# Attention and quantised FFN on one core: K's and Q's products ahead of the scores in the first five units, 27 turns of the identity instead of 30

## The chip, the core and the metric

The kernel runs on one core of one Trainium2 chip. The metric is the device time of one execution in microseconds (us). The core has five engines that run side by side, each taking its own instructions strictly in the order in which they stand: PE (TensorE, matmuls, with PEld for its weight loads), DVE (VectorE), ACT (ScalarE), POOL (GpSimd) and SP, which here issues all DMA transfers. Engines wait for each other through semaphores.

## The reference

The input x has 16 sequences of 256 tokens with 256 channels. One attention layer and one feed-forward layer follow, each with a layer norm before and after it and a residual. Cut to what matters here:

```python
x = x + layernorm(attn(layernorm(x)))     # 16 heads of 128, causal
    q = einsum('bpd,hde->bphe', x, W_Q) + b_Q      # the same for k, v
    scores = einsum('bqhe,bkhe->bhqk', q, k) / sqrt(128), masked above the diagonal
    z = einsum('bkhe,bhqk->bqhe', v, softmax(scores))
    out = einsum('bqhe,hed->bqd', z, W_O) + b_O
x = x + layernorm(ffn(layernorm(x)))      # gate, up, down, weights in 4-bit codes with scales
```

The results are wanted in float32 accuracy. The kernel gets it from TensorE's faster float32r format by splitting each operand into a high part and a low part (high = value rounded to float32r, low = value minus high) and adding three products: high x high, high x low, low x high.

## The kernel before, in words

**Tiles.** The 4096 tokens are worked in 8 blocks of 512 (two sequences each). Per block there are 8 pairs of heads, so 16 heads; one head in one block is a *unit*, and there are 128 units. After all units come the groups of the feed-forward layer. This case plays in the first units.

**What a unit u does**, stage by stage (the functions stand below):
- `st_qk` (L370): K's product `pk` (six matmuls of 128x512) and Q's product `pq` (six more). ACT copies from them `kh`, `kr`, `qh`, `qr` (with bias), DVE makes the low parts `kl`, `ql`. `pk` and `pq` have one PSUM buffer each: the next unit's `pk` waits until this unit's `kl` has read the old one, the next `pq` until `ql` has.
- `st_s` (L421): the scores, ten matmuls into two buffers `sc` (one for each sequence); DVE adds the mask and takes the row minimum `mn` (four instructions, with an accumulator read after each); then come the low parts of V that are waiting in the list `after` (L442); ACT takes four exponentials `pr` with their sums, DVE reciprocals `rc`, POOL scales `pr`. The next unit's scores need the two `sc` buffers, which the exponentials read last.
- `st_t` (L460): DVE's transpose `tr` within 32x32 squares, which waits for POOL's scaled `pr`; `st_w` and `st_b` (L471, L475) send it to DRAM (`hop`) and fetch it back (`pt`), which completes the transpose.
- `st_v` (L402): V's product `pv` for four heads at once; units 0 to 3 of each half block make the four parts. For the first two, ACT copies `vh` and the subtraction that gives `vl` is put into the list `after`, that is, it is issued on DVE by the *next* unit's `st_s`, behind its mask instructions. For the other two ACT copies `vr`. `pv` has one PSUM buffer.
- `st_p`, `st_z`, `st_o`: the splits `ph` and `pl` of `pt`, the product with V (`pz`), and the product with W_O (`po`).

**Weights.** Raw weights of a pair (`raw`, six buffers) are split once, in block 0, by `w_split` (L297): ACT writes the high part, DVE (for `wk`, `wq`) or POOL (for `wv`, `wo`) the low part; the splits are stored to DRAM and fetched back in later blocks. `w_split` also asks for the next pair's raw weights. `w_get` (L331) puts a split into the list `splits`; `slot` (L133) takes one job from such a list at fixed points of the loop, only a job of the kinds that it is asked for, and only the first of the list.

**Order.** `run` (L95) issues every compute instruction behind all earlier ones, so the order in which the Python code calls is the order on each engine; `dma` (L86) does the same for SP. At most eight transfers are under way, since each reuses the semaphore of the eighth before it.

**The start.** PE first turns the identity 30 times into an unused buffer (`keep_warm(30)`, L992), then transposes block 0's normalised tokens (`tpx`, with 3 and 6 more turns), and the loop of L1006 begins at i = -5. In step i the loop works on unit i+4's scores, unit i+5's K and Q, unit i's `pz`, and so on. Before step -5 the splits of pair 2 of V and pair 1 of K and Q are in the list (L998). Thus the order on PE in the first units is: pk0 pq0, sc0, pk1 pq1, pv0, sc1, pk2 pq2, pv1, sc2, ... (the number is the unit).

Of the kernel before, what the change touches and what calls it, by code (L numbers as in the profile page):

```python
# [28 lines left out]
def kernel(  # L29
# [30 lines left out]
    def f(ap):  # L60
        return ap.bitcast(F32)
# [43 lines left out]
    V_, G_, A_, N_ = "vgan"  # L105
    urgent, behind, splits, idle, made, spare = (deque() for _ in range(6))
# [18 lines left out]
    def add(jobs, job, kind):  # L125
        jobs.append([job, 0, kind])

    def overdue(time):
        while late and late[0][0] <= time:
            _, do, args = late.popleft()  # L130
            do(*args)

    def slot(kinds, *lanes):  # L133

        now[0] += 1
        overdue(now[0])
        for jobs in lanes or (splits, urgent, behind, made, spare, idle):
            if step(jobs, kinds):
                return
# [149 lines left out]
    def w_tile(n):  # L289
        return wp.tile([P, 2, 1024 if n == "v" else 512], F32R, tag=f"w{n}", name=f"w{n}", bufs=2)  # L290
# [36 lines left out]
    def split(p, n):  # L327
        w_split(p, n)
        yield from ()

    def w_get(p, n):  # L331

        if p < NG:
            add(splits, split(p, n), A_ if n in "vo" else V_)
        elif p < len(pairs):
            overdue(now[0] + 4)
            if n == "v":
                key, part = p // 2, p % 2
                w = HALF.pop(key) if part else w_tile(n)
                HALF[key] = w  # L340
                dma(f(w[:, part]), WD[key % (NG // 2), n][:, part])
                if part:
                    W[key, n] = w_view(HALF.pop(key))
            else:
                w = w_tile(n)
                dma(f(w), WD[p % NG, n])
                W[p, n] = w_view(w)
# [16 lines left out]
    N = len(units)  # L364
# [5 lines left out]
    def st_qk(i):  # L370
        b, g, j = units[i]
        h = 2 * g + j
        await_(ready, (1, b), urgent)
        await_(W, (i // 2, "k"), splits)
        await_(W, (i // 2, "q"), splits)
        xt = XT[1, b]
        wk_, wq_ = W[i // 2, "k"], W[i // 2, "q"]
        cols = slice(j * E, (j + 1) * E)
        pk = ps.tile([P, TB], F32, tag="pk", name="pk")
        mm3(pk, [(lambda a, kt=kt: wk_[:, a, kt, cols], lambda c, kt=kt: xt[:, c, kt, :]) for kt in range(2)], MOVING_LAST, lows_last=True)  # L380
        kh = work.tile([P, TB], F32R, tag="kh", name="kh")
        kl = work.tile([P, TB], F32R, tag="kl", name="kl")
        kr = work.tile([P, 2, P], F32, tag="kr", name="kr")
        bias = bqk[:, 1, h : h + 1]
        run(nc.scalar.activation, kh, pk, AF.Identity, bias=bias)
        run(nc.scalar.activation, kr, pk.rearrange("p (a c) -> p a c", a=2)[:, :, 0:P], AF.Identity, bias=bias)
        run(nc.vector.scalar_tensor_tensor, kl, pk, bias, f(kh), ALU.add, ALU.subtract)
        K[i] = (kh, kl, kr)

        pq = ps.tile([P, TB], F32, tag="pq", name="pq")  # L390
        mm3(pq, [(lambda a, kt=kt: wq_[:, a, kt, cols], lambda c, kt=kt: xt[:, c, kt, :]) for kt in range(2)], MOVING_LAST, lows_last=True)
        qh = work.tile([P, 2, P], F32R, tag="qh", name="qh")
        ql = work.tile([P, 2, P], F32R, tag="ql", name="ql")
        qr = work.tile([P, 2, P], F32, tag="qr", name="qr")
        bias = bqs[:, h : h + 1]
        pq2 = pq.rearrange("p (a c) -> p a c", a=2)
        run(nc.scalar.activation, qh, pq2[:, :, P:], AF.Identity, bias=bias)
        run(nc.scalar.activation, qr, pq2[:, :, 0:P], AF.Identity, bias=bias)
        run(nc.vector.scalar_tensor_tensor, ql, pq2[:, :, P:], bias, f(qh), ALU.add, ALU.subtract)
        Q[i] = (qh, ql, qr)  # L400
# [70 lines left out]
    def st_w(u):  # L471
        HOP[u] = dram.tile([P, 4, 6 * 32], F32, tag="hop", name="hop", bufs=4)
        spread(HOP[u], TR.pop(u).rearrange("p k m i -> p k (m i)"))
# [218 lines left out]
    def x_ops(sb):  # L692

        xr = []
        for b in (2 * sb, 2 * sb + 1):
            xr.append(wide("xr"))
            dma(xr[-1], HOP2[b])
        yield A_, 8

        def block(kt, bb):  # L700
            return xr[bb].rearrange("p a (m i) -> p m a i", m=8)[:, 4 * kt : 4 * kt + 4]

        def four(ap):
            return ap.rearrange("p (t a i) -> p t a i", t=4, a=4)

        ops = X[sb] = {}

        def put(name, hi, lo, src):
            run(nc.scalar.copy, four(hi), src)
            run(nc.gpsimd.tensor_tensor, four(lo), src, f(four(hi)), ALU.subtract)  # L710
            ops[name] = hi, lo

        def pair():
            t = work.tile([P, 2, 2, TB], F32R, tag="xT", name="xT", bufs=4)
            return [(t[:, 0, k], t[:, 1, k]) for k in range(2)]

        def less(o, a, b):
            run(nc.gpsimd.tensor_tensor, o, a, b, ALU.subtract)

        x11, x12, x21, x22 = block(0, 0), block(0, 1), block(1, 0), block(1, 1)  # L720
        p1, p2 = pair()
        put("11", *p1, x11)
        yield A_
        put("21", *p2, x21)
        yield G_
        t1, t3, t4 = x11, x12, x21
        less(t1, x12, x11)
        yield G_
        less(t3, x22, x12)
        yield G_  # L730
        t2 = four(sb_tile("raw", "xsum", 6))
        less(t2, x22, t1)
        yield A_
        p1, p2 = pair()
        put("t2", *p1, t2)
        yield G_
        less(t4, t2, x21)
        yield A_
        put("t1", *p2, t1)
        yield A_  # L740
        w = w_tile("k")
        put("t3", w[:, 0], w[:, 1], t3)
        yield A_
        w = w_tile("q")
        put("22", w[:, 0], w[:, 1], x22)

        def last_one():
            hi = work.tile([P, TB], F32R, tag="ph", name="xh")
            lo = work.tile([P, TB], F32R, tag="pl", name="xl")
            put("t4", hi, lo, t4)  # L750

        if sb == 0:

            ops["last"] = last_one
        else:
            yield A_
            last_one()
# [230 lines left out]
    def keep_warm(count):  # L988
        for n in range(count):
            run(nc.tensor.transpose, warm[:, n % 4, :], ident, ident)  # L990

    keep_warm(30)  # L992
    add(urgent, first, V_)
    finish(urgent)
    run(nc.gpsimd.tensor_scalar, bqs, bqk[:, 0, :], qscale, 1.0, ALU.mult, ALU.mult)
    for p in range(2):
        w_split(p, "v")
    for p, n in (2, "v"), (1, "k"), (1, "q"):  # L998
        w_get(p, n)

    def weights(*of):
        for pn, n in of:
# [3 lines left out]
    for i in range(-5, N + 2):  # L1006
        p = i // 2
        odd = i % 2 == 1
        if p >= 0 and not odd and p < len(pairs):
            b, g = pairs[p]  # L1010
            if g == 0 and b + 1 < NBLK:
                add(urgent, ln1(b + 1), N_)
            if b == 0 and g == 6:
                pieces = [(fg, n) for fg in range(NG) for n in "gud"]
                f_load(*pieces[0])
            if b == 0 and g == 7:
                for m, piece in enumerate(pieces):
                    add(idle, f_make(*piece, pieces[m + 1] if m + 1 < len(pieces) else None), V_)
            if b == NBLK - 1 and g == 0:
                add(spare, x_ops(0), N_)  # L1020
        if 0 <= i + 4 < N:
            st_s(i + 4)
        slot(V_)
        if i + 5 < N:
            st_qk(i + 5)
        slot(V_, urgent, behind)
        slot(G_)
        slot(G_)
        if 0 <= i + 4 < N:
            st_t(i + 4)  # L1030
        if i == N:
            X[0].pop("last")()
        if i >= N - 4:
            part(0, ("m1", "m2", "m6", "m5", "m7", "m3")[i - (N - 4)])
        if 0 <= p - 1 < len(pairs):
            st_o(p - 1, i % 2)
        if 0 <= i < N:
            st_z(i)
        if 0 <= i + 1 < N:
            st_p(i + 1)  # L1040
        if 0 <= i + 4 < N:
            st_v(i + 4)
        elif after:
            run(*after.popleft())
        if 0 <= i + 3 < N:
            st_b(i + 3)
        if 0 <= i + 4 < N:
            st_w(i + 4)
        if odd:
            weights((p + 1, "o"), (p + 5, "v"))  # L1050
        else:
            weights((p + 4, "k"), (p + 4, "q"))
        slot(A_ + G_)
        if N - 9 <= i < N - 7:
            f_get(0, "ug"[i - (N - 9)])
# [97 lines left out]
```

## Time and profile before

| what | value |
|---|---|
| three timed runs | 1523.2, 1522.82, 1521.78 us; median 1522.82 |
| the profiled execution's own time | 1522.04 us |
| its span in the profile | 1520.3 us |
| PE busy | 1501.7 us (99% of the span), 7831 matmuls |
| DVE, ACT, POOL busy | 1175.9 (77%), 1033.9 (68%), 810.3 us (53%) |
| PE busy in the first five stretches of 10 us | 8.36, 8.57, 7.19, 9.52, 9.28 us |
| PE busy from 50 to 60 and from 60 to 80 us | 10.00 and 20.00 us |
| PE busy in the last 21 us | 12.44 us |
| share of DMA busy from 10 to 50 us, by 10 us | 0.85, 0.89, 0.99, 0.97 |

How to read it: an engine's busy time is the time in which it has an instruction under way. The timeline gives, for each group of equal instructions, its start, its length in us, engine, line, operation, tiles, sizes and count, and in brackets the idle time before it with what ended that idle time. Nearly all instructions carry L99, the line of the helper `run`, so groups are told by their tiles. Instructions overlap by some tenths of a microsecond on one engine: the distance from start to start is what an engine takes for one, the length is what the next engine has to wait for.

### The profile page before, as it was taken

The page shows a single profiled execution, that of the slowest core. Times are in us where ns is not written, and L with a number is a line of the kernel's source. Part 1 is how long each engine was busy: PE and PEld are TensorE (multiplying, and loading weights), DVE is VectorE, ACT ScalarE, POOL GpSimd, SP SyncE. Part 2 cuts the span into 40 slices and gives each one's busy share as a digit, 9 for nine tenths or more (in the row PEclk, how much of TensorE's full clock was granted, in tenths as well). Part 3 has the DMA queues.
Part 4 walks back from the last instruction along what each step waited for, and adds up shares of the span by engine and source line. Part 5 has one row for each costly group of instructions (what it writes and reads, how often), then busy time and mean ns, then how long its engine had stood idle before and what let it go on. Part 6 is the DMA issues. An engine that isn't in the chain of part 4 may idle for free.

```text
span 1520.3 us, 25782 instructions
## 1 busy us (share of the span) xinstructions
PE 1501.7 (99%) x7831; PEld 1278.5 (84%) x7831; DVE 1175.9 (77%) x2950; ACT 1033.9 (68%) x2606; POOL 810.3 (53%) x1018
## 2 busy tenths in 40 slices
PE   8999999999999999999999999999999999999997
PEld 7888888888888888888888888887788878878886
DVE  6876787787787888788778777777877777787766
ACT  6886776777676677676776767675666665666565
POOL 3754578677667776866876876882320230140100
PEclk9999999999999999999999999999999999999999
DMA  8998899999889899899899999976547465645551
GB/s 287 336 317 266 263 310 298 294 299 317 281 291 329 280 322 311 265 322 299 280 287 304 312 304 316 310 247 254 219 180 276 185 232 195 254 174 201 216 232 57
DMA packets 200427, 407.55 MB, mean 268 GB/s; under 512 B 21472, under 2 KB 128480, under 8 KB 189536
## 3 DMA queue, kind: packets, MB, share of 16 engines
q1 hardware_dynamic: 200288, 405.91, 79.6%
q8 instruction: 62, 1.02, 0.3%
q14 instruction: 77, 0.63, 0.1%
HBM read 294.15 MB, written 111.67 MB: 267 GB/s over the span
## 4 chain that ended last, share of the span: by engine, by line
PE 89%; DVE 5%; ACT 4%; DMA 1%; issue 1%; POOL 1%; POOLq 0%; ACTq 0%; SPq 0%; DVEq 0%
PE pd L99 11%; PE pk L99 11%; PE po L99 11%; PE pv L99 11%; PE pq L99 11%; PE pz L99 10%; PE sc L99 9%; PE pa L99 7%; PE pf L99 5%; DVE sum L99 3%; PE pe L99 2%; DVE inter L99 1%; ACT inter L99 1%; ACT part L99 1%; ACT o L99 1%
## 5 line engine op out<-in xcount | busy, mean ns | idle before, releaser
L99 POOL TENSOR_SCALAR pr<-pr,rc 128x128 f32<-128x128 f32 (+1 forms) x512 | 250.2, 504 | 89.9 <-DVE rc L99 89.9
L99 ACT ACTIVATE pr<-sc,mn 128x128 f32<-128x128 f32 (+1 forms) x512 | 208.2, 419 | 87.2 <-DVE mn L99 87.0
L99 POOL TENSOR_TENSOR pl<-pt,ph 128x512 fp32r<-128x512 f32 x128 | 165.0, 1289 | 190.1 <-ACT ph L99 181.8
L99 DVE CUSTOM_DVE_ANT_0 sc<-sc,mask 128x128 f32<-128x128 f32 (+1 forms) x512 | 180.6, 373 | 67.8 <-PE sc L99 59.1
L99 PE MATMUL pv<-wv,xT 128*128 128x512 f32 x768 | 208.9, 407 | 0.0
L99 PE MATMUL pd<-inter,wd 128*128 128x512 f32 (+1 forms) x792 | 199.7, 386 | 2.7 <-DVE inter L99 1.4
L99 ACT ACTIVATE zh<-pz,bqk 128x512 fp32r<-128x512 f32 x128 | 88.3, 690 | 167.3 <-PE pz L99 167.2
L99 PE MATMUL pk<-xT,wk 128*128 128x512 f32 x768 | 199.4, 395 | 0.3 <-POOL xT L99 0.2
L99 PE MATMUL pq<-xT,wq 128*128 128x512 f32 x768 | 196.3, 391 | 0.0
L99 POOL TENSOR_TENSOR rs<-rs,mhalf 128x4 f32<-128x4 f32 (+1 forms) x35 | 35.9, 1026 | 283.9 <-DVE rs L99 277.5
L99 PEld LDWEIGHTS pd<-inter,wd 128*128 128x128 f32 x792 | 144.2, 188 | 38.6 <-DVE inter L99 6.5
L99 PEld LDWEIGHTS pq<-xT,wq 128*128 128x128 f32 x768 | 144.2, 188 | 32.8
L99 PE MATMUL po<-zh,wo 128*128 128x512 f32 x512 | 157.7, 389 | 0.0
L99 PEld LDWEIGHTS pk<-xT,wk 128*128 128x128 f32 x768 | 134.9, 188 | 23.8 <-POOL xT L99 0.7
L99 PEld LDWEIGHTS pv<-wv,xT 128*128 128x128 f32 x768 | 135.0, 189 | 23.6
L99 ACT COPY part<-pa 128x512 f32<-128x512 f32 x192 | 111.5, 584 | 62.7 <-PE pa L99 60.3
L99 DVE SCALAR_TENSOR_TENSOR zl<-pz,bqk,zh 128x512 fp32r<-128x512 f32 x128 | 95.8, 749 | 73.7 <-ACT zh L99 73.6
L99 ACT CAST inter<-sum 128x512 fp32r<-128x512 f32 x128 | 80.1, 626 | 100.0 <-DVE sum L99 99.9
L99 DVE TENSOR_TENSOR inter<-sum,inter 128x512 fp32r<-128x512 f32 x128 | 93.2, 728 | 58.9 <-ACT inter L99 56.0
L99 DVE STREAM_TRANSPOSE tr<-pr 128x768 f32<-128x768 f32 x128 | 123.3, 963 | 1.7 <-POOL pr L99 1.2
L99 DVE SCALAR_TENSOR_TENSOR kl<-pk,bqk,kh 128x512 fp32r<-128x512 f32 x128 | 96.1, 751 | 30.7 <-ACT kr L99 26.7
L99 PEld LDWEIGHTS po<-zh,wo 128*128 128x128 f32 x512 | 96.0, 188 | 19.9
(138 smaller groups left out, 3779.6 us busy)
## 6 DMA issues: line engine op xcount, KB each, us to landing
hop<-tr SPq DMA_DIRECT2D x512, 96.0 KB
pt<-hop SPq DMA_DIRECT2D x128, 384.0 KB
wk<-wk SPq DMA_DIRECT2D x64, 512.0 KB
wq<-wq SPq DMA_DIRECT2D x64, 512.0 KB
wo<-wo SPq DMA_DIRECT2D x64, 512.0 KB
wu<-fu SPq DMA_DIRECT2D x32, 1024.0 KB
wg<-fg SPq DMA_DIRECT2D x32, 1024.0 KB
wv<-wv SPq DMA_DIRECT2D x56, 512.0 KB
```

Source lines behind the costliest of these rows:

```text
L99: ins = op(dst, *args, **kw)
```

## The change

1. `keep_warm(30)` becomes `keep_warm(27)`.
2. In steps i = -5 to -1, `st_qk(i + 5)` is called ahead of `st_s(i + 4)` and not behind it. Right behind it two slots take jobs from `splits` alone, so that the next pair's `wk` and `wq` are split behind the copies of K and Q.
3. The split of V's pair 2 is not put into the list at the start, ahead of K's and Q's; it is put there in step -4. Its copy on ACT now stands behind the first unit's exponentials and `vh`.

From step 0 on, the order on the compute engines is that of before.

```diff
-    keep_warm(30)
+    keep_warm(27)
...
-    for p, n in (2, "v"), (1, "k"), (1, "q"):
-        w_get(p, n)
+    for n in "kq":
+        w_get(1, n)
...
+        if i < 0:
+            st_qk(i + 5)
+            for _ in range(2):
+                slot(V_, splits)
         if 0 <= i + 4 < N:
             st_s(i + 4)
         slot(V_)
-        if i + 5 < N:
+        if 5 <= i + 5 < N:
             st_qk(i + 5)
...
             st_w(i + 4)
+        if i == -4:
+            w_get(2, "v")
```

The order on the engines of the changed kernel, first units (the number is the unit, for weights the pair):

```
PE   pk0 pq0 pk1 pq1 sc0 pv0 pk2 pq2 sc1 pv1 pk3 pq3 sc2 pv2 pk4 pq4 sc3 pv3 sc4 pk5 pq5 pz0 ...
ACT  kh0 kr0 qh0 qr0 wk1 wq1 kh1 .. qr1 exp0 vh0 wv2 kh2 .. qr2 wk2 wq2 exp1 vh1 wv3 kh3 .. qr3 exp2 vr2 kh4 .. qr4 wk3 wq3 exp3 ...
DVE  kl0 ql0 wk1 wq1 kl1 ql1 mask0 rc0 tr0 kl2 ql2 wk2 wq2 mask1 vl0 rc1 tr1 kl3 ql3 mask2 vl1 rc2 tr2 kl4 ql4 wk3 wq3 mask3 ...
```

On SP the third and second raw loads of K and Q go ahead of V's store and the first `hop`; the count of transfers is the same.

## The prediction

> **What bounds the kernel.** I read the page first: who is busy, and the chain that ended last.
>
> ```profile
> PE 1501.7 (99%) x7831; PEld 1278.5 (84%) x7831; DVE 1175.9 (77%) x2950; ACT 1033.9 (68%) x2606; POOL 810.3 (53%) x1018
> ...
> PE 89%; DVE 5%; ACT 4%; DMA 1%; issue 1%; POOL 1%; POOLq 0%; ACTq 0%; SPq 0%; DVEq 0%
> ```
>
> TensorE carries the chain. So a change of order can only move PE's idle time: 1520.3 - 1501.7 = 18.6 us, of which 8.6 lie in the last 21 us (21.0 - 12.44 busy), untouched here. The second view is PE's timeline over the first 50 us. Its brackets (idle, and what ended it) show gaps ahead of the scores `sc` of units 0, 1, 2 and 4: 0.99, 2.18, 1.06, 1.12 us, 5.35 in all; from unit 5 on PE has none for a long time.
>
> ```profile
> 18.04 1.52 PE L99 MATMUL pv<-wv,xT 128*128 128x512 f32 x6
> 21.75 0.49 PE L99 MATMUL sc<-kr,qr 128*128 128x128 f32 x2 [2.18 <-ACT qr L99]
> ...
> 23.06 1.53 PE L99 MATMUL pk<-xT,wk 128*128 128x512 f32 x6
> 24.43 1.52 PE L99 MATMUL pq<-xT,wq 128*128 128x512 f32 x6
> 25.79 1.52 PE L99 MATMUL pv<-wv,xT 128*128 128x512 f32 x6
> ```
>
> To see: the scores of unit 1 wait for `qr`, ACT's last copy; and between `sc` and the next `pv` PE has `pk` and `pq` to do, 2.7 us. The third view is ACT's timeline: it shows why `qr` is late.
>
> ```profile
> 13.40 0.47 ACT L99 ACTIVATE qr<-pq,bqs 128x256 f32<-128x256 f32 x1
> 16.75 0.63 ACT L99 ACTIVATE wv<-rawv 128x512 fp32r<-128x512 f32 x1 [2.88 <-DMA rawv<-in_wv]
> 17.29 0.35 ACT L99 ACTIVATE pr<-sc,mn 128x128 f32<-128x128 f32 x1
> ```
>
> The split of V's pair 2 blocks ACT until its transfer lands at 16.7, and the exponentials, the weight splits and unit 1's copies queue behind it. The fourth view is DVE's timeline around unit 1's scores:
>
> ```profile
> 23.02 0.27 DVE L99 CUSTOM_DVE_ANT_0 sc<-sc,mask 128x128 f32<-128x128 f32 x1
> ...
> 24.15 0.43 DVE L99 CUSTOM_DVE_ANT_0 sc<-sc,mask 128x256 f32<-128x256 f32 x1
> ...
> 24.50 0.69 DVE L99 TENSOR_TENSOR vl<-pv,vh 128x512 fp32r<-128x512 f32 x1
> ```
>
> `vl` of unit 0 stands behind unit 1's mask instructions and ends at 25.19. `pv` has one buffer, so unit 1's `pv` may not start before that. It starts at 25.79, and nobody waits: `pk` and `pq` lie between.
>
> **The change, part by part.**
>
> *Three turns fewer.* Thirty turns take 7.84 - 1.56 = 6.28 us. Turn by turn the trace has them 0.213 apart up to 7.59, then 0.11, as the four transposes after them (8.28 - 7.84 over 4): the clock rose at about 7.6. PE turns without a break, so it should rise at the same moment. What comes three places earlier comes 3 x 0.11 = 0.33 us earlier; the tokens `xn` are ready at 7.34 at the latest, so they don't hold it. If the rise counts turns and not time, nothing is gained; if it were all slow turns, 3 x 0.21 = 0.64. I take -0.33.
>
> *K and Q first, V's split later.* I walk through the new order with the rows of before, start to start: `pk`, `pq`, `pv` 1.37 each (results 0.15 later), `sc` 1.15; ACT `kh` 0.57, `kr`, `qh`, `qr` 0.36 each, `wk` or `wq` 0.52, `wv` 0.54, the exponentials of a unit 1.58, `vh` 0.48; DVE `kl` 0.73, `ql` 0.40, a weight's low part 0.60, the mask group 1.48 (its first exponential may start 0.90 after it), `vl` 0.60, `tr` 0.89; POOL's scaling 0.81 twice; 0.05 for each handover. Done on the old order this gives scores of units 0 to 4 at 13.8, 21.8, 28.5, 34.1, 40.7, where the trace has 13.92, 21.75, 28.38, 34.03, 40.72. On the new order:
>
> | step on PE | start | released by | idle, start to start |
> |---|---|---|---|
> | pk0, pq0 | 9.6, 11.0 | copies of the tokens | |
> | pk1, pq1 | 13.1, 14.4 | `kl0` ends 13.0 | 0.7 |
> | sc0, pv0, pk2, pq2 | 15.8, 17.0, 18.3, 19.7 | | 0 |
> | sc1 | 21.1 | | 0 |
> | **pv1** | **26.6** | `vl0` | **4.4** |
> | pk3, pq3, sc2 | 28.0, 29.4, 30.7 | | 0 |
> | **pv2** | **34.4** | `vl1` | **2.6** |
> | pk4, pq4, sc3, pv3 | 35.8, 37.2, 38.5, 39.7 | | 0 |
> | sc4 | 43.2 | exponentials of unit 3 | 2.1, and 0.2 within |
> | sc5, sc6 | 50.3, 57.6 | `ql5`, `ql6` | 0.5, 0.8 |
>
> The row that decides is pv1. What was two products behind `sc1` now follows it directly, while `vl0` still stands on DVE behind unit 1's masks. And those come late: ACT's exponentials of unit 0 run from 18.2 to 19.8, then `vh0`, `wv2`, the four copies of unit 2 (to 22.4), `wk2` and `wq2` (to 23.7); DVE follows with `kl2`, `ql2`, both low parts to 24.4, masks to 25.9, `vl0` to 26.6. PE has finished `sc1` at 22.3. Queued behind `pv1` on PE are `pk3`, `pq3` and the scores of unit 2, so ACT and DVE then wait for PE in turn, and `pv2` meets the same ring. At step 0 the old order returns: `sc4` comes right behind `pv3`, with the exponentials of unit 3 not yet read.
>
> The wait for V's transfer is really gone: `wv2` is needed at 20.3 and landed at 16.7. The early weights are hidden too: POOL and DVE free their buffers at about 12.4 and 14.6, four to six microseconds before the old 18.8 and 20.3 at which SP issued these loads, and ACT wants them at 22.4. DMA is 85 to 99% busy from 10 to 50 us, but the first two `pt` landed at 33.1 and 40.7 and were read at 40.5 and 46.7, and all uses come later. So these edits cost nothing; the cover is that slack.
>
> Sum without the clock: `sc4` 43.2 against 40.72 is +2.5; its second half, `sc5` and `sc6` add 0.2 + 0.5 + 0.8 = 1.5. From unit 7 on PE also has `po`: its scores come 7.8 us apart (61.85, 69.68) and leave ACT and DVE time to catch up. The lag ends there and nothing is won back, since PE is the bound. +4.0, the three turns included. With handovers of 0.02 to 0.08 it is +3.8 to +4.3.
>
> *The clock.* A gap of 4.2 us (4.4 less the overlap of ends) is longer than any before. What such a gap does is seen at the end of the program:
>
> ```profile
> 1512.66 0.82 PE L99 MATMUL tpo<-ident,oT 128*128 128x128 f32 x4 [0.40 <-ACT oT L99]
> ```
> ```profile
> 1514.00:1516.00 2.00, 0.00 (x0) 0.00 (x0) 1.94 (x10) 0.97 (x3) 0.70 (x1) 1.00 0.41 138
> 1516.00:1518.00 2.00, 0.00 (x0) 0.00 (x0) 0.68 (x2) 1.12 (x3) 0.00 (x0) 0.59 0.45 146
> ```
>
> (Columns: stretch, length, busy PE, PEld, DVE, ACT, POOL, granted clock, DMA share, GB/s.) The last matmul ends at 1513.48. A mean of 0.59 is full clock for 0.36 us and 0.50 after: the clock fell at 1516.36, 2.9 us after the last work. The 2.18 us gap at 19.6 did not do it. 4.2 lies beyond 2.9, so I take a fall. How long it stays down: 2.9 us at least, as the fall took; at most 6.0, since at the start PE turned from 1.56 to 7.6 before it rose. At half clock, half of that is lost: 1.5 to 3.0, middle 2.25, and the ring of `pv2` passes it on in full. Nothing, if it does not fall; twice 3.0 if the 2.4 us at pv2 do it again.
>
> [...]
>
> **Forecast: 1522.04 + 4.0 + 2.25 = 1528.3 us**, against the profiled execution's own time. That execution is 0.8 under the median of the runs (1522.82), within their 1521.78 to 1523.2.
>
> **Rivals.**
> - *The stall without a fall of the clock*: 1522.04 + 4.0 = 1526.0. For it: 2.2 us left the clock alone, and only one row shows a fall. Chance 0.30; one in five of these would lie within 0.2%.
> - *Faster*: `vl0` done before PE is through with `sc1`. Then neither `pv` waits, 4.4 + 2.6 go, and 4.0 - 7.0 gives 1519.0. It decides at 22.3 us: `vl0` would have to end 4.3 us earlier than walked. For it: ACT no longer waits 2.88 us for a transfer. Against: even a DVE free at 22.0, when the scores appear, needs 1.48 + 0.69 for masks and `vl`, so 2 us stay. Chance 0.07.
> - *A wash*: the gaps removed (5.35 by the brackets) and the gaps added cancel, as when masks are not held up by `wk2` and `wq2`: pv1 costs 2 and the rest shrinks alike. 1522 to 1523. Chance 0.07.
> - *A late transfer*: `rawk`, `rawq` of pair 2 landing 5.2 us after issue, as `rawv` did (11.55 to 16.7), still come by 20. If they come after 22.4, each microsecond goes into pv1's wait: 1530. Chance 0.06.
>
> The forecast has 0.50. A measurement of this kernel can tell about 0.2% (3 us) from no change. Faster 0.07; same 0.07 + 0.06 = 0.13; slower 0.80. The range leaves out the faster and most of the same cases below, and takes in 4.3 + 6.0 above: 1525.0 to 1532.3.
>
> **What would show it.** In the changed profile PE's timeline should have [4 <-DVE vl] ahead of unit 1's `pv` near 22 to 27 us, about 2.4 ahead of unit 2's, about 2 ahead of `sc4`; no [2.88 <-DMA] on ACT's `wv`; `tpx` starting near 7.4; matmuls of `pv`, `pk` behind the first gap with twice their length if the clock fell; sameness after some 60 us. It is wrong if `pv` of unit 1 follows `sc1` closely, or if the first 60 us show no later start of equal units.

## The result, and the profile after

| | before | after |
|---|---|---|
| median of four runs | 1522.34 us (1521.78 to 1523.2) | 1531.04 us (1529.52 to 1531.25) |
| profiled execution, span | 1522.04, 1520.3 us | 1529.52, 1527.7 us |
| PE busy | 1501.7 us | 1505.2 us |
| mean granted clock | 0.999 | 0.996 |

The change makes the kernel slower by 8.7 us: ratio 1.0056, with a 95% interval of [1.0043, 1.0068]. The profiled execution of the changed kernel is the fastest of its four, 1.5 us under their median; against the profiled execution of the kernel before it is 7.5 us slower, and its span 7.4 us longer. The forecast was 1528.3, the range 1525.0 to 1532.3.

The page of the changed kernel, busy times and chain that ended last:

```profile
PE 1505.2 (99%) x7828; PEld 1281.3 (84%) x7828; DVE 1176.8 (77%) x2950; ACT 1034.8 (68%) x2606; POOL 809.5 (53%) x1018
...
PE 90%; DVE 5%; ACT 3%; issue 1%; POOL 1%; DMA 0%; POOLq 0%; ACTq 0%; DVEq 0%
```

To see: PE has three instructions fewer and is busy 3.5 us *longer*. Added waiting alone can't do that; matmuls have become slower somewhere. The other 3.9 of the span's 7.4 us are idle time.

PE's timeline of the changed kernel, in which I look for the brackets and for groups longer than before:

```profile
20.68 0.38 PE L99 MATMUL sc<-kr,qr 128*128 128x128 f32 x2
...
26.20 2.34 PE L99 MATMUL pv<-wv,xT 128*128 128x512 f32 x6 [4.21 <-DVE vl L99]
28.34 2.46 PE L99 MATMUL pk<-xT,wk 128*128 128x512 f32 x6
30.64 1.55 PE L99 MATMUL pq<-xT,wq 128*128 128x512 f32 x6
...
35.81 1.80 PE L99 MATMUL pv<-wv,xT 128*128 128x512 f32 x6 [2.47 <-DVE vl L99]
37.40 2.76 PE L99 MATMUL pk<-xT,wk 128*128 128x512 f32 x6
...
46.42 0.49 PE L99 MATMUL sc<-kr,qr 128*128 128x128 f32 x2 [2.11 <-ACT pr L99]
...
48.33 2.69 PE L99 MATMUL pk<-xT,wk 128*128 128x512 f32 x6
```

To see: three gaps, and behind each of them `pv` or `pk` at up to 2.76 us where before it took 1.52. DVE's timeline of the changed kernel shows what the first gap waits for:

```profile
23.36 0.69 DVE L99 SCALAR_TENSOR_TENSOR wq<-rawq,wq 128x512 fp32r<-128x512 f32 x1
23.96 0.29 DVE L99 CUSTOM_DVE_ANT_0 sc<-sc,mask 128x128 f32<-128x128 f32 x1
...
25.11 0.43 DVE L99 CUSTOM_DVE_ANT_0 sc<-sc,mask 128x256 f32<-128x256 f32 x1
...
25.46 0.68 DVE L99 TENSOR_TENSOR vl<-pv,vh 128x512 fp32r<-128x512 f32 x1
```

To see: `vl` of unit 0 stands behind pair 2's `wq` and unit 1's masks and ends at 26.14; `pv1` starts at 26.20. The same three stretches by the granted clock (columns: stretch, length, busy PE, PEld, DVE, ACT, POOL, granted clock, DMA share, GB/s):

```profile
24.00:28.00 4.00, 1.80 (x6) 1.41 (x7) 2.34 (x13) 1.72 (x8) 1.62 (x4) 0.87 0.89 218
28.00:32.00 4.00, 4.00 (x14) 3.21 (x13) 0.97 (x2) 2.17 (x4) 1.28 (x1) 0.71 1.03 411
32.00:36.00 4.00, 1.53 (x12) 1.30 (x11) 3.33 (x12) 2.31 (x9) 0.08 (x1) 1.00 1.01 344
36.00:40.00 4.00, 4.00 (x13) 3.11 (x13) 1.15 (x2) 0.83 (x3) 1.55 (x4) 0.65 0.56 197
...
48.00:52.00 4.00, 4.00 (x14) 3.25 (x14) 2.71 (x11) 2.53 (x11) 3.40 (x5) 0.65 0.86 260
```

The trace's clock records give the edges: half clock (0.50 granted) from 26.92 to 30.33, from 37.16 to 40.57 and from 47.40 to 50.81, each time 3.41 us; such a drop to half clock is called a *fall* below. From unit 7 on nothing more changes: its scores start at 69.04 instead of 61.69 (by PE's timeline; the prediction's 61.85 is from the chain), +7.35 of the +7.4 of the span.

### The profile page after: what moved, and what is told of

Its sections match the earlier page's. It is cut to its first block, busy times and chain, and to the rows that moved or that the text cites. A ratio compares the mean times of both kernels' runs of the same rounds, so it can differ in the third digit from the quotient of the medians.

```text
span 1527.7 us, 25776 instructions
## 1 busy us (share of the span) xinstructions
PE 1505.2 (99%) x7828; PEld 1281.3 (84%) x7828; DVE 1176.8 (77%) x2950; ACT 1034.8 (68%) x2606; POOL 809.5 (53%) x1018
## 4 chain that ended last, share of the span: by engine, by line
PE 90%; DVE 5%; ACT 3%; issue 1%; POOL 1%; DMA 0%; POOLq 0%; ACTq 0%; DVEq 0%
PE pk L99 12%; PE pv L99 11%; PE pq L99 11%; PE pd L99 11%; PE po L99 11%; PE pz L99 10%; PE sc L99 9%; PE pa L99 7%; PE pf L99 5%; DVE sum L99 3%; PE pe L99 2%; DVE inter L99 1%; ACT inter L99 1%; ACT part L99 1%; ACT o L99 1%
## 5 line engine op out<-in xcount | busy, mean ns | idle before, releaser
L99 PE MATMUL pk<-xT,wk 128*128 128x512 f32 x768 | 202.9, 400 | 0.9 <-DVE kl L99 0.6
```

What stands on the lines that cost most here:

```text
L99: ins = op(dst, *args, **kw)
```

## The experiments

Theory: (a) the gaps at `pv1`, `pv2` and `sc4` are what the prediction's walk through the new order found, `vl` behind the next unit's masks and `sc4` right behind `pv3`, worth about 4; (b) the clock falls after them, worth the rest. Rival to (a): not the place of `vl` on DVE but ACT's queue, or late transfers. Rival to (b): slow matmuls from busy memory, not from idle time. Each run stands beside runs of the kernel before on its own chip; differences are of medians.

### Gaps kept, PE kept busy in them (e1_fill)

The changed kernel, with turns of the identity into the unused buffer in the three gaps:

```diff
+    FILL = {-3: 38, -2: 22}
...
+        if i in FILL:
+            keep_warm(FILL[i])
...
             st_v(i + 4)
...
+        if i == 0:
+            keep_warm(18)
         if 0 <= i + 4 < N:
             st_s(i + 4)
```

> The changed kernel, with 38, 22 and 18 extra turns of the identity on TensorE, placed in the three gaps: ahead of unit 1's pv, ahead of unit 2's pv, ahead of unit 4's scores. They write an unused buffer, so nothing waits for them but TensorE itself, and the waits for vl and for the exponentials stay as they are. Theory (the order on DVE makes the gaps, and the falls of the clock behind them make the rest): the clock stays at 1.00 through the first 60 us, the gaps stay in time, and the time is 1522.3 + 4.0 = 1526.3 us, some 4 to 5 under the changed kernel. Rival (the loss over 4 us comes from the later engines or from transfers, and the low clock is a by-product without a price): the time stays at 1530 to 1531.

Measured: 1526.83 (1526.31 to 1527.52), +5.1, ratio 1.003 [1.0019, 1.0041]. PE's timeline, and the windows of this kernel:

```profile
22.13 4.31 PE L99 MATMUL warm<-ident 128*128 128x128 f32 x38
26.51 1.67 PE L99 MATMUL pv<-wv,xT 128*128 128x512 f32 x6
```
```profile
24.00:28.00 4.00, 3.93 (x29) 3.44 (x28) 2.63 (x12) 1.72 (x8) 1.37 (x4) 1.00 0.75 189
28.00:32.00 4.00, 4.00 (x24) 3.49 (x23) 1.83 (x3) 3.01 (x6) 1.55 (x2) 1.00 1.03 368
```

`pv1` starts no earlier, but takes 1.67 instead of 2.34, and the clock stays at 1.00 with DMA as busy as in the changed kernel (1.03 in both). So the slow matmuls come from idle time. Of 8.7 us some 3.6 belong to the clock and 5.1 to the gaps.

### `vl` ahead of the masks (e2_vl_now), and that with filled gaps (e6_vl_now_fill)

The changed kernel, with `vl` of units 0 and 1 issued right behind `vh`, no longer through the list `after`; e6 adds 17 turns in the gap ahead of `pv2` and 20 in the one ahead of `sc4`:

```diff
-            after.append((nc.vector.tensor_tensor, vl[:, bi], pv, f(vh[:, bi]), ALU.subtract))
+            low = (nc.vector.tensor_tensor, vl[:, bi], pv, f(vh[:, bi]), ALU.subtract)
+            if k < 2:
+                run(*low)
+            else:
+                after.append(low)
```

> The changed kernel, with vl of units 0 and 1 issued on DVE right behind its vh, and no longer behind the next unit's masks. Theory (pv of unit 1 and 2 wait for vl, and vl waits for the masks): the 4.2 us gap ahead of unit 1's pv shrinks to about 0.4; unit 2's pv still waits about 2 for vl, which now stands behind a transpose; unit 4's scores wait about 3 for the exponentials. 1522.3 + 0.8 = 1523.1 without a fall of the clock, to 1526 with one or two. Rival (the late copies on ACT, with the weight splits behind them, make the gap, wherever vl stands): a gap of 3 us or more stays ahead of unit 1's pv or moves to unit 2's scores, and the time stays over 1528.

Measured for e2: 1523.79 (1522.61 to 1526.06), +2.0, 1.0013 [1.0003, 1.0022]. Its waits on PE (us in total, times, longest), where the changed kernel has 6.7, 2, 4.2 in the first row:

```profile
PE pv L99 <- DVE vl L99: 2.2, 2, 1.9
PE sc L99 <- ACT pr L99: 2.1, 1, 2.1
```

`pv1`'s gap falls from 4.21 to 0.29, `pv2`'s from 2.47 to 1.86; one fall of the clock is left (29.74 to 33.15). Moving one subtraction, in two units, takes back 6.7 of 8.7 us, its share of the falls included. So it was its place on DVE, and not ACT's queue or a transfer.

> vl of units 0 and 1 right behind vh, as in the second experiment, and 17 and 20 turns in the two gaps that were left there (ahead of unit 2's pv and of unit 4's scores), so that the clock has no reason to fall. Theory (walk of the order alone): 1521.8 + 0.8 = 1522.6 us, 1 to 1.5 under the second experiment, and its executions scatter less than that one's 1522.6 to 1526.1. Rival (its scatter has another source than the clock): median and scatter stay.

Measured for e6: 1522.96 (1522.27 to 1525.54), +0.7, 1.0006 [0.9997, 1.0015]. The mean granted clock of the profiled execution is 0.999, as in e1, and the median is where it was expected. But two of ten executions still took 1525.5. Their mean granted clock is 0.999 like that of the other eight, so falls of the clock are not what made them slow, and their source stays open. Of e2's two executions at 1526 this can't be said: their means are 0.997 and 0.996, at the low end of the 0.996 to 0.998 of its ten.

### V's split later, alone (e3_v_later); 27 turns, alone (e4_27_turns); both (e8_v_later_27)

The kernel before with part 3 of the change, with part 1, and with both, but without part 2:

```diff
-    keep_warm(30)
+    keep_warm(27)            # e4 and e8
...
-    for p, n in (2, "v"), (1, "k"), (1, "q"):
-        w_get(p, n)
+    for n in "kq":           # e3 and e8
+        w_get(1, n)
...
+        if i == -4:
+            w_get(2, "v")
```

> The kernel before, with the third part of the change alone: V's pair 2 is split in step -4, behind the first exponentials and vh, and K and Q stay behind the scores. Theory (ACT's wait of 2.88 us for V's transfer is what makes unit 1's copies late, and this part of the change is good by itself): unit 1's scores wait about 1 us and not 2.2, the other gaps stay, and the time is 1522.3 - 1.7 = 1520.6 us. Rival (the split of V costs ACT the same 0.54 us wherever it stands, and the wait was hidden): 1522 to 1523. A second rival (it is this part that loses, since wv2 now stands ahead of unit 2's copies): over 1524.

Measured for e3: 1520.28 (1519.45 to 1521.51), -1.5, 0.9987 [0.9978, 0.9997]. Unit 1's scores, which waited 2.18 us before:

```profile
19.13 0.49 PE L99 MATMUL sc<-kr,qr 128*128 128x128 f32 x2 [0.22 <-ACT qr L99]
```

The wait is shorter than expected (about 1 us): with V's split gone from the head of the list, ACT does the split of pair 1's `wk` already at 10.56, ahead of unit 0's copies, so that only `wq` stands between unit 0's exponentials and unit 1's copies.

> The kernel before with 27 turns in place of 30, nothing else. Theory (the clock rises by time, not by turns; the three turns that go are fast ones): -0.3 us, 1522.0, less than the runs scatter; in the profile the first transposes start 3 x 0.11 to 3 x 0.21 us earlier, as the moment of the rise lets them. Rival (the rise is put off by fewer turns): no gain, or up to 0.7 lost.

Measured for e4: 1521.6 (1520.58 to 1522.82), -0.2, 0.9996 [0.9986, 1.0005]. Not to be told from nothing. In its profiled execution the first transposes start 1.47 us earlier (6.37 against 7.84), not the 0.3 to 0.6 that were expected, since the clock rose at 5.30 there and not at 7.65.

> The kernel before with the two parts of the change that the runs found harmless or good: V's split later, and 27 turns. Theory (the two add up): 1521.8 - 1.5 - 0.2 = 1520.1 us, the fastest of all. Rival (with the wait for V's transfer gone, an earlier start only lengthens another wait): 1520.3 or more.

Measured for e8: 1520.08 (1519.58 to 1521.09), -2.15, 0.9985 [0.9977, 0.9994]: parts 1 and 3 without part 2 are better than both kernels. The gain was in the change, and part 2 covered it. That the time is the expected 1520.1 is partly chance: the kernel before stood at 1522.23 on this chip, not at 1521.8.

### K and Q early in two steps only (e7_two_early)

The changed kernel, with its new order only in steps -5 and -4, so that PE has `pk` and `pq` between the masks and `pv` from there on:

```diff
-        if i < 0:
+        if i < -3:
             st_qk(i + 5)
...
-        if 5 <= i + 5 < N:
+        if 2 <= i + 5 < N:
             st_qk(i + 5)
```

> The changed kernel with the early K and Q in steps -5 and -4 alone, so for units 0 and 1; from step -3 on the old order, with pk and pq between the scores and pv. Theory (the early products hurt where they leave pv right behind the scores, and help nothing by themselves, since the wait moves to the two score buffers): no gap of 2 us is left; unit 1's scores wait 0.8 for the exponentials, its pv 0.9 for vl, unit 2's scores 1.8; 1521.8 - 1.2 = 1520.6 us, no better than the V split's move alone. Rival (early K and Q are good wherever they stand, and only their number was too large): under 1519.5.

Measured: 1521.47 (1520.4 to 1522.92), -0.8, 0.9993 [0.9984, 1.0002]. Its waits on PE in the first 70 us:

```profile
PE sc L99 <- ACT qr L99: 2.6, 2, 1.5
...
PE sc L99 <- ACT pr L99: 0.6, 1, 0.6
PE pv L99 <- DVE vl L99: 0.6, 1, 0.6
PE pk L99 <- DVE kl L99: 0.6, 1, 0.6
```

Short waits in other places, no better than e3: the early products themselves bring nothing here. Against e8 on the same chip, which has all but them, they cost 1.4 us by the medians.

### One gap filled, or two (e5_fill_first, e10_fill_second, e9_fill_two)

The edit of e1 with some of its three counts of turns: 38, 0, 0 in e5; 0, 22, 0 in e10; 38, 22, 0 in e9. They ask what each fall costs.

> The changed kernel with 38 extra turns of the identity in the first gap alone, ahead of unit 1's pv; the gaps of about 2.5 us ahead of unit 2's pv and 2.1 ahead of unit 4's scores stay empty. [...]

Measured for e5: 1526.59 (1525.98 to 1527.66), +4.4, 1.0027 [1.0017, 1.0037]. I had expected falls behind the second and the third gap in most executions, and about 1529; with the clock at full it would be e1's 1526.8. In the profiled execution the second gap, 2.5 us as in the changed kernel, stayed without a fall, and the third fall cost nothing that shows:

```profile
40.00:44.00 4.00, 1.90 (x9) 1.39 (x8) 2.96 (x12) 2.31 (x10) 0.78 (x2) 0.88 0.78 257
44.00:48.00 4.00, 4.00 (x17) 3.50 (x17) 2.62 (x10) 2.53 (x10) 3.40 (x6) 0.70 0.84 283
```

The clock is below 1.00 only here, behind the gap at `sc4`; yet from `pk0` to the scores of unit 6 it takes 48.91 us, as in e1 (48.81). The eight executions lie in two groups, 1526.0 to 1526.1 and 1527.0 to 1527.7. One fall of 3.41 us takes 0.001 off the mean granted clock (half of 3.41 in a span of 1524.3). That mean is 0.998 to 0.999 in the lower group and 0.998, 0.998, 0.998 and 0.997 in the upper, so the upper group as a whole does not have a fall more than the lower. A fall behind the second gap in place of the one behind the third would fit both; only one execution was profiled, so this is not shown.

> The changed kernel with 38 and 22 turns in the first and second gap, none in the third (ahead of unit 4's scores). Theory, mended after the fifth experiment (a fall behind the third gap is nearly free, since the scores of units 5 and 6 wait for ACT and DVE anyway): before + 4.0 to 4.4, as with the first gap alone filled, but without that one's executions 1.2 to 1.7 us above the others. Rival (the third fall costs 1.7 as well, and the fifth experiment's executions had none): before + 5.7.

Measured for e9: 1526.93 (1526.53 to 1527.63), +4.3, 1.0031 [1.0019, 1.0043]. PE's timeline of e9, and then of e1, in which the third gap is filled too:

```profile
43.61 0.49 PE L99 MATMUL sc<-kr,qr 128*128 128x128 f32 x2 [2.10 <-ACT pr L99]
...
45.46 2.75 PE L99 MATMUL pk<-xT,wk 128*128 128x512 f32 x6
...
51.98 0.38 PE L99 MATMUL sc<-kr,qr 128*128 128x128 f32 x2
```
```profile
50.78 0.49 PE L99 MATMUL sc<-kr,qr 128*128 128x128 f32 x2 [0.24 <-ACT qr L99]
...
58.12 0.49 PE L99 MATMUL sc<-kr,qr 128*128 128x128 f32 x2 [0.57 <-ACT qr L99]
```

To see: in e9 `pk` takes 2.75 us, since the clock has fallen (mean 0.58 from 44 to 48 us); the scores of unit 5 then start without a wait, and those of unit 6 at 58.42, 0.3 behind e1's. In e1 PE waits for `qr` there. The slow clock only fills waits that PE would have had, so the third fall is nearly free.

> The changed kernel with 22 turns in the second gap alone; the first gap of 4.2 us stays empty, and so does the third. Theory (the first fall costs half of one window of 3.4 us, all of it on the path, the third nothing): before + 4.2 + 1.7 = +5.9 in nearly all executions. Rival (the first fall alone makes the whole difference between filled and changed kernel, as the copies behind it set everything later): before + 8.

Measured for e10: 1528.43 (1528.17 to 1531.98), +5.8, 1.0045 [1.0031, 1.0059]. The first fall is back:

```profile
24.00:28.00 4.00, 1.95 (x6) 1.54 (x7) 2.34 (x12) 1.72 (x8) 1.62 (x4) 0.82 0.88 226
28.00:32.00 4.00, 4.00 (x16) 3.20 (x15) 0.96 (x2) 2.17 (x4) 1.29 (x1) 0.75 1.02 407
```

It costs 5.8 - 4.3 = 1.5 us against e9, nearly half of the 3.41 us that each fall of the changed kernel lasted. Three executions lie within 0.3 us; two lie 2.4 and 3.5 above the median. The profiled one is one of these (1530.85), and it lost its time elsewhere: between 1000 and 1200 us, in the feed-forward layer, PE is idle 4.3 us, where e9 has 1.9; 2.5 of the 4.3 are two waits for transfers of weights, `wg` and `wu`.

### The sum

| part | from | us |
|---|---|---|
| gaps, 27 turns and the V split taken together | e9 - before | +4.3 |
| first fall of the clock | e10 - e9 | +1.5 |
| second fall, and what is not separated | after - e10 | +2.9 |
| all | | +8.7 |

From `pk0` to the scores of unit 6 the profiled executions take 43.86 (before), 48.81 (e1, no fall), 49.08 (e9, the third only), 50.35 (e10, the first only) and 52.22 us (after, all three): gaps 4.95, third fall 0.3, first 1.5, second and third together 1.9. So about 1 of the 2.9 us stays open; the scatter between executions is as large.

Where that scatter arises can be read off the profiled executions. From the scores of unit 7 to those of the last unit, at about 1002 us, the distance to the kernel before changes by no more than 0.02 us in any of them: 7.35 (after), 4.4 (e1), 4.5 (e9), 5.5 (e10), -2.6 (e3), -1.55 (e4). Behind that, in the feed-forward layer, it changes by 0.1 us (after) to 3.2 (e10, to 8.7); e4's -1.55 shrinks to -0.2 there. So the first units set a shift that lasts, and a single execution's total can hide it by a microsecond or more.

## Why the prediction was right, and where it was not

- *PE bounds, only its idle time can move.* Right for idle time, incomplete: 3.5 of the 7.4 us are added busy time of PE itself, from matmuls at half clock. A slip that nothing rests on: the 12.44 us busy belong to the stretch from 1500 us to the end of the span, 20.3 us and not 21, so the end holds 7.8 us of idle time and not 8.6.
- *The walk.* Right in its order, in what each wait ends on, and nearly in size. Idle ahead of `pk1`, `pv1`, `pv2` and `sc4`: walked 0.7 (start to start), 4.2, 2.4, 2.1; measured 0.57, 4.21, 2.47, 2.11. `pv1` was walked to 26.6 and started at 26.20, `sc1` 21.1 and 20.68, 0.4 early, because the whole start was (below). In e1, where the clock stays up, `sc4` starts at 43.60 (walked 43.2), and the short waits at `sc5` and `sc6` are there, 0.24 and 0.57 (walked 0.5 and 0.8). From `pk0` to the scores of unit 6 the walk has 48.0 us (57.6 - 9.6) and e1 48.81, so it was 0.8 too short. Sum: +4.0 walked; +4.3 (e9) to +5.1 (e1) measured.
- *The order is what does it.* Right: `vl0` ended at 26.14 and `pv1` started 0.06 later; taken ahead of the masks (e2), 6.7 of 8.7 us come back.
- *V's transfer no longer waited for, early weights hidden.* Right: no wait for a transfer of weights stands on PE in the first 70 us. As a term of its own, that wait was worth -1.5 (e3).
- *Three turns: -0.33.* The first transposes start at 6.92 instead of 7.84, 0.92 earlier, since in this execution the clock also rose earlier, at 6.44 and not at 7.65. "It should rise at the same moment" doesn't hold from one execution to another. By time, e4 gives -0.2, within its uncertainty.
- *The clock, +2.25.* This is the term that was mis-sized. The prediction priced one fall, and had "Nothing, if it does not fall; twice 3.0 if the 2.4 us at pv2 do it again". It did fall again, and a third time at `sc4`. Each fall lasted 3.41 us, near the lower end of the 2.9 to 6.0 allowed. The first cost 1.5 us, the second and third together 1.9, of which the third is some 0.3. By the medians the clock cost 3.6 (8.7 - 5.1, e1) to 4.4 us (8.7 - 4.3, e9). What failed is the reading of the one row: from "2.9 us after the last work" I made a delay that a gap has to outlast, and so cleared gaps of 2.1 to 2.5 us. The section on the hardware has the same delay in the changed kernel beside it: 4.4 us.
- *The sum.* In the profiled execution the start gave -0.92 (forecast -0.33), the gaps 4.95 (4.33) and the clock 3.4 (2.25): 7.4 against 6.25. That the clock's term is not further off is luck: one fall too dear at 2.25 stood for three cheaper ones, and an early start took off part of the rest.
- *The rivals.* "The stall without a fall" priced at 1526.0 is nearly e1 (1526.8, no fall) and e9 (1526.9, the third fall alone), which had to be built. "Faster" needed `vl0` done at 22.3; it ended at 26.14. The wash does not occur, and no transfer was late.

## What to carry to other kernels

When products are moved ahead, ask what stood between the reader that frees a buffer and the buffer's next use: here `pk` and `pq` covered 2.7 us between `sc` and `pv`, and with them gone a subtraction that was late for nobody held up PE. Where PE is the bound, a gap on it costs its length, and here up to some 1.5 us more where the clock fell, for the matmuls behind it, unless these would have waited anyway (0.3). Price the parts of a change one by one: a gain of 2 us (e8) lay inside a loss of 8.7.

## What the runs showed of the hardware

**The edges of the clock.** By the clock records the changed kernel has a rise at 6.44 us and falls at 26.92, 37.16 and 47.40, each 3.41 us long at a granted 0.50. The distances from edge to edge, 20.48, 10.24 and 10.24 us, are 6, 3 and 3 times these 3.41. Before, the clock rises at 7.65, and the fall at the end of the program, which the prediction worked out as 1516.36, stands at 1516.34. It comes 2.9 us after the last matmul (1513.48); in the changed kernel the fall at the end, at 1525.37, comes 4.4 us after it (1521.01). So the 2.9 us were not a fixed delay.

**PE was at work in part of the 3.41 us ahead of each fall in the first units.** PE's idle share of the 3.41 us that end at a fall can be worked out from the timeline. The first one in the changed kernel goes from 26.92 - 3.41 = 23.51 to 26.92, and PE is idle in it until 26.20: 79%. The second and third come to 60% and 62%. In e5, e9 and e10 falls followed 61, 62 and 85%; in e2 one followed 55%. The length of a gap does not tell by itself: in the changed kernel falls came after gaps of 2.47 and 2.11 us, while the 2.18 us gap of before, e5's second, 2.5 us, and e10's third, 2.1 us, brought none in the profiled executions. So a gap of some 2 us cost or did not cost here, and in the changed kernel the three falls came 0.72, 1.35 and 0.98 us after work had begun again.

**The mean clock is lower in executions with falls.** It is 0.999 in the profiled runs without a fall in the first units, 0.998 in those with one (e2, e5, e9, e10) and 0.996 with three (after). The four executions of the changed kernel have 0.995 to 0.997, so by these means the clock fell in all of them. Of the 69 executions of the kernel before that stand beside the experiments, 46 have 0.998 or 0.997, and 23 have 0.999; in e3 and e8, where the 2.18 us gap is gone, 18 of 21 have 0.999. So that the 2.18 us gap left the clock alone, on which the prediction leaned, holds for the one profiled execution, and by these means most likely not for most others; none of the others was profiled. The times of those with 0.998 and 0.999 do not differ by more than 0.4 us in the median on any chip.

**The start scatters with the rise of the clock.** PE works from 1.56 us on, and the clock rose at 5.30 us in e4, at 6.44 in the changed kernel and at 7.65 before. Turns ahead of the rise take twice as long (0.21 us against 0.11), and the first transposes start at 6.37, 6.92 and 7.84 us. In five runs with the same 27 turns (e4, e10, after, e1, e9) they start at 6.37, 6.75, 6.92, 7.22 and 7.25, a spread of 0.88 us, more than three turns take (0.33 to 0.64).
